# A first-chunk head for each pass, weights behind the input, head steps at slot ends, and one more product in 32 on GpSimd

## The chip, the cores and the metric

The kernel runs on one core of a Trainium2 chip. The core has TensorE (PE) for matmuls, VectorE (DVE), ScalarE (ACT) and GpSimd (POOL) for elementwise work, SyncE (SP) that here issues all DMAs, an on-chip memory of 128 partitions (SBUF), and eight PSUM banks into which TensorE writes. Each engine takes its own instructions in order. The metric is device time in microseconds, lower is better.

## The reference

Two layers on x of shape (1, 64, 256, 128) = (b, c, t, f). Layer 0 is a two-directional Mamba, first along t (each f is a sequence), then along f (each t is a sequence):

```python
def _mamba(u, p):
    x, z = split(u @ in_proj_w.T)                  # 128 channels each
    x = silu(causal_depthwise_conv4(x) + conv_b)
    dt, B, C = split(x @ x_proj_w.T, [4, 20])
    dt = softplus(dt @ dt_proj_w.T + dt_proj_b)
    A = -exp(A_log)                                # 128 channels x 16 states
    h[t] = exp(dt[t] * A) * h[t-1] + dt[t] * B[t] * x[t]
    y[t] = sum_s h[t] * C[t] + x[t] * Dp
    return (y * silu(z)) @ out_proj_w.T
def _block(u, p): return _mamba(rmsnorm(u, norm_w), p) + u
xt = xt + concat(block_fwd(xt), flip(block_bwd(flip(xt)))) @ tlin_w + tlin_b
xf = xf + concat(block_fwd(xf), flip(block_bwd(flip(xf)))) @ flin_w + flin_b
```

Layer 1 is a global layer norm and a two-directional convolutional LSTM over windows of 8 time steps, a transposed convolution, two PReLUs and a residual. Everything is float32.

## The kernel before

**Two passes and a third stage.** `Stage` runs twice (stage 0 along t, stage 1 along f); `ConvLstm` follows. Between them the whole tensor `X` (128 partitions x 128 x 128) stays in SBUF. A pass has 64 chunks of 512 tokens, each with two directions d. Of the 128 channels x 16 states, one 128x1024 tile holds an eighth (a "pair" of 128x512), so a chunk has 2 x 8 = 16 pairs. A pair is a **slot** S; there are 16 x 64 = 1024 slots in a pass and 2048 in all.

**What a slot does.** `inputs` (L445) spreads dt·x over states on TensorE into a PSUM tile `bx` (three buffers of two banks). `decays` (L462 to L468) computes exp(dt·A) into `dA` on ScalarE, from a tile `rep` to which a DMA of 512 KB (L420) has copied each channel's dt 16 times. `times_b` multiplies `bx` by B; `recur` is the scan on VectorE (L490); `outputs` multiplies by C on GpSimd (L503); `add_up` sums the states on TensorE into the bank `y` (L512). For most slots `times_b` is on VectorE (L480). For a slot in `SWAPPED` (modulo 32; there are seven) ScalarE first copies `bx` to the SBUF tile `dA` (L462), the decays go into the PSUM tile, and B is multiplied on GpSimd (L477). The edges of `dA` are set to zero by small ScalarE copies (L465) where a tile changes its role or its direction.

**The order.** `Stage.run` writes the order out by hand. In slot S it emits B for S+1, the scan of S, C for S-1, the spread for S+2, the decays for S+2 (at one slot S+2 and S+3), then the **head steps** listed for the slot in `HEAD`, then `add_up` of S-2 and, at slots 2 and 3 of a chunk, the closing products and `keep` of the chunk before.

**The head.** Everything that a chunk needs before its first scan is a list of steps with slots, relative to 16 slots before the chunk starts: load `u`, its squares, means and rms; `normalise` (GpSimd, L311), whose result four DMAs bring into the padded tile `unp` (L314); `project_x` and `project_z` for both directions; all silus together between two loads of ScalarE's function tables; `project_bc`, whose result goes out to DRAM (`away`) and comes back as B and C; softplus in three steps (`pv`, `e`, `w`, `lw`, summed by TensorE and copied to `dt`); `dt_away` and `spread_dt`, which bring it back as `rep`; `times_x`. All of the head's matmuls, the closing ones and `made` share one PSUM bank (`mm`, tag "mm"), which passes on when its reader is done. The first chunk of a pass takes the same steps with no slot beside them.

**The start.** `Mamba.__init__` (L160 to L229) loads all weights with 33 transfers and builds the matrices, `Gates.load` (L690 to L694) issues 9 more, and then the first chunk's `u` is loaded.

**`made`.** During chunks of the second pass, the response of the LSTM's input weights to the norm's gain and bias is computed: at slot 10, `fetch` loads 512 KB of weights, and at slot 6 of ten chunks `respond` (L707) multiplies them, 8 matmuls of 2 columns (16 instructions in the trace), and ScalarE copies the result (L710).

Of the kernel before, what the change touches and what calls it, by code (L numbers as in the profile page):

```python
# [37 lines left out]
C = 64  # L38
# [20 lines left out]
NREP = 7  # L59
NH = 5  # L60
LAG = 2
SWAPPED = (3, 5, 10, 14, 19, 26, 29)
# [7 lines left out]
    (-11, "load"),  # L70
    (-7, "squares"),
    (-5, "means"),
    (-5, "rms"),
    (-3, "normalise"),
    (0, "project_x", 0),
    (1, "project_z", 0),
    (4, "project_x", 1),
    (5, "project_z", 1),
    (5, "silus"),
    (6, "project_bc", 0),  # L80
    (8, "softplus_a", 0),
    (8, "softplus_b", 0),
    (10, "spread_bc", 0, 0),
    (10, "softplus_sum", 0),
    (12, "dt_away", 0),
    (12, "spread_bc", 0, 1),
    (12, "spread_dt", 0, 0),
    (12, "times_x", 0),
    (12, "spread_dt", 0, 1),
    (12, "project_bc", 1),  # L90
    (12, "spread_dt", 0, 2),
    (13, "softplus_a", 1),
    (13, "softplus_b", 1),
    (14, "spread_dt", 0, 3),
    (15, "spread_dt", 0, 4),
    (15, "softplus_sum", 1),
    (15, "spread_dt", 0, 5),
    (15, "spread_dt", 0, 6),
    (15, "spread_bc", 1, 1),
    (18, "dt_away", 1),  # L100
    (18, "spread_dt", 0, 7),
    (19, "spread_dt", 1, 0),
    (20, "spread_bc", 1, 0),
    (20, "spread_dt", 1, 1),
    (20, "times_x", 1),
    (22, "spread_dt", 1, 2),
    (22, "spread_dt", 1, 3),
    (23, "spread_dt", 1, 4),
    (26, "spread_dt", 1, 5),
    (27, "spread_dt", 1, 6),  # L110
    (27, "spread_dt", 1, 7),
# [3 lines left out]
class Mamba:  # L115


    def __init__(self, ctx, tc, d):
        nc = tc.nc
        self.nc, self.tc = nc, tc  # L120
        cp = ctx.enter_context(tc.tile_pool(name="m_const", bufs=1))

        self.ident = cp.tile([P, P], F32, name="ident")
        make_identity(nc, self.ident)

        mask = cp.tile([P, 2, NK, DL], F32, name="mask")
        flat = mask.rearrange("p r k d -> p (r k d)")
        nc.vector.tensor_add(flat, self.ident[:, 0:C], self.ident[:, C:P])  # L130
        self.sel = cp.tile([P, 2, NK, P], F32, name="sel")
        for r in range(2):
            for k in range(NK):
                nc.vector.tensor_copy(
                    self.sel[:, r, k].rearrange("p (s d) -> p s d", s=NS),
                    mask[:, r, k].unsqueeze(1).to_broadcast([P, NS, DL]),
                )
        self.fold = cp.tile([P, NK, 32], F32, name="fold")
        with tc.tile_pool(name="m_fold", bufs=1, space=PSUM) as ps:
            pf = ps.tile([P, NK, 32], F32, name="pf")  # L140
            for k in range(NK):
                nc.tensor.matmul(
                    pf[:, k], lhsT=self.sel[0:32, 0, k], rhs=self.ident[0:32, 0:32], start=True, stop=True
                )
            nc.vector.tensor_copy(self.fold, pf)


        self.ones = cp.tile([P, P], F32, name="ones")
        nc.vector.memset(self.ones, 0.0)
        for h in range(2):  # L150
            own = slice(h * C, (h + 1) * C)
            nc.vector.memset(self.ones[own, own], 1.0 / C)
        self.eps = cp.tile([P, 1], F32, name="eps")
        nc.vector.memset(self.eps, RMS_EPS)

        self.cb = cp.tile([P, 4], F32, name="cb")
        self.dtb = cp.tile([P, 4], F32, name="dtb")
        self.dp = cp.tile([P, 4], F32, name="dp")
        normw = cp.tile([C, 4], F32, name="normw")
        nc.sync.dma_start(out=self.cb, in_=d["conv_b"])  # L160
        nc.sync.dma_start(out=self.dtb, in_=d["dt_b"])
        nc.sync.dma_start(out=self.dp, in_=d["Dp"])
        nc.sync.dma_start(out=normw, in_=d["norm_w"])


        nc.scalar.preload_act_table_set(EXP_AND_LN)
        self.A = cp.tile([P, 4, NG], F32, name="A")
        nc.sync.dma_start(out=self.A, in_=d["A_log"])
        nc.scalar.activation(self.A, self.A, AF.Exp)
        nc.vector.tensor_scalar(self.A, self.A, -1.0, None, ALU.mult)  # L170

        self.G1, self.G2, self.Wz, self.Wdt, self.Wbc, self.W2 = ([] for _ in range(6))
        self.W3, self.lin_b = [], []
        with tc.tile_pool(name="m_prep", bufs=2) as pp, tc.tile_pool(
            name="m_prep_ps", bufs=2, space=PSUM
        ) as ps:
            lins = []
            for i, n in enumerate(("tlin", "flin")):
                lin = pp.tile([C, 2, C], F32, name=n, tag=n, bufs=1)
                nc.sync.dma_start(out=lin, in_=d[n + "_w"].rearrange("(h i) o -> i h o", h=2))  # L180
                lins.append(lin)
                b = cp.tile([C, 1], F32, name=n + "b", tag=n + "b")
                nc.sync.dma_start(out=b, in_=d[n + "_b"].rearrange("(c o) -> c o", o=1))
                self.lin_b.append(b)

                w3 = cp.tile([P, 2, C], F32, name=f"w3{i}", tag=f"w3{i}")
                nc.vector.memset(w3, 0.0)
                nc.vector.tensor_add(w3[0:C, 0], lin[:, 0], lin[:, 1])
                nc.vector.tensor_add(w3[0:C, 0], w3[0:C, 0], self.ident[0:C, 0:C])
                nc.vector.tensor_copy(w3[C:P, 1], w3[0:C, 0])  # L190
                self.W3.append(w3)

            for i in range(4):
                win = pp.tile([C, 2 * P], F32, name="win", tag="win")
                nc.sync.dma_start(out=win, in_=d["in_proj"][i])
                cw = pp.tile([C, 4, P], F32, name="cw", tag="cw")
                nc.sync.dma_start(out=cw, in_=d["conv_w"][i].partition_broadcast(C))
                xpd = pp.tile([RANK, P], F32, name="xpd", tag="xpd")
                nc.sync.dma_start(out=xpd, in_=d["x_proj_dt"][i])
                dtw = pp.tile([RANK, P], F32, name="dtw", tag="dtw")  # L200
                nc.sync.dma_start(out=dtw, in_=d["dt_proj"][i])
                xbc = cp.tile([P, NBC], F32, name=f"xbc{i}", tag=f"xbc{i}")
                nc.sync.dma_start(out=xbc, in_=d["x_proj_bc"][i])
                self.Wbc.append(xbc)
                ow = pp.tile([C, P], F32, name="ow", tag="ow")
                nc.sync.dma_start(out=ow, in_=d["out_proj"][i])

                nc.vector.tensor_scalar(win, win, normw[:, i : i + 1], None, ALU.mult)
                wz = cp.tile([C, P], F32, name=f"wz{i}", tag=f"wz{i}")
                nc.vector.tensor_copy(wz, win[:, P : 2 * P])  # L210
                self.Wz.append(wz)

                taps = ((3, 2), (1, 0)) if i % 2 == 0 else ((2, 3), (0, 1))
                for j, keep in enumerate((self.G1, self.G2)):
                    g = cp.tile([P, P], F32, name=f"g{j}{i}", tag=f"g{j}{i}")
                    nc.vector.tensor_mul(g[0:C], win[:, 0:P], cw[:, taps[j][0]])
                    nc.vector.tensor_mul(g[C:P], win[:, 0:P], cw[:, taps[j][1]])
                    keep.append(g)

                pw = ps.tile([P, P], F32, name="pw", tag="pw")  # L220
                nc.tensor.matmul(pw, lhsT=xpd, rhs=dtw, start=True, stop=True)
                wdt = cp.tile([P, P], F32, name=f"wdt{i}", tag=f"wdt{i}")
                nc.vector.tensor_copy(wdt, pw)
                self.Wdt.append(wdt)

                po = ps.tile([P, C], F32, name="po", tag="po")
                nc.tensor.matmul(po, lhsT=ow, rhs=lins[i // 2][:, i % 2], start=True, stop=True)
                w2 = cp.tile([P, C], F32, name=f"w2{i}", tag=f"w2{i}")
                nc.vector.tensor_copy(w2, po)  # L229
                self.W2.append(w2)  # L230


class Stage:
# [8 lines left out]
    def __init__(self, ctx, m, stage, L, X, src, moments, gates):  # L242
# [24 lines left out]
        self.at = {}  # L267
# [8 lines left out]
    def mm(self, name):  # L276
        return self.ps_mm.tile([P, NTOK], F32, name=name, tag="mm")
# [40 lines left out]

    def project_x(self, ch, d):
        nc, m, L = self.nc, self.m, self.L  # L320
        i = 2 * self.stage + d
        first, second = (3, 1) if d == 0 else (4, 6)
        px = self.mm("px")
        xs = self.wk.tile([P, NTOK], F32, name="xs", tag="xs", bufs=3)
        nc.tensor.matmul(self.seqs(px), lhsT=m.G1[i], rhs=self.unp[:, :, first : first + L], start=True, stop=False)  # L325
# [99 lines left out]
    def head(self, ch):  # L425
        todo = {}
        for slot, name, *args in HEAD:
            todo.setdefault(slot, []).append((getattr(self, name), (ch, *args)))
# [736 lines left out]
```

## Time and profile before

| | |
|---|---|
| median of three runs | 7435.62 us (7434.42 to 7440.39) |
| the profiled execution | 7439.22 us, span 7437.4 us |
| busy: PE, DVE, ACT, POOL | 6526, 6987, 6000, 6559 us |
| first scan of the first pass | 72.0 us after the start |
| last scan of the first pass, first of the second | 3338.2 (two in a row, 4.45 us), 3395.3 us |
| last scans of the second pass | 6739.9 us (two in a row, 4.45 us) |
| end | 7437.4 us |

A line of a group gives line, engine, operation, tiles and shapes, the count, then the busy time in us and the mean in ns, then the engine's idle time just before and who ended it. A line of a table of stretches gives from, to and length in us, the busy time of each engine with its instructions, the TensorE clock that was granted (1.00 is full speed), the DMA engines' busy share, and GB/s. A line of waits gives who waited for whom, us in total, times, and the longest. A line of the timeline gives start and duration in us, engine, line, operation, and in brackets the idle time before it and who ended it.

An engine's instructions overlap a little at their ends, so that the distance between two starts is somewhat less than the mean duration: a scan with B behind it starts 2.20 us before that B (2000 to 2110 us), though its row says 2.27.

### The profile page before, as it was taken

To read this page: it belongs to the slowest core of one execution; us is meant where nothing else is said; L and a number is where in the kernel's file an instruction comes from. 1 tells how busy PE (TensorE), PEld (TensorE's weight loads), DVE (VectorE), ACT (ScalarE), POOL (GpSimd) and SP (SyncE) were. 2 spreads that over 40 slices of the span, in tenths; PEclk is the share of its full clock that TensorE was granted. 3 is DMA by queue.
4 is the path that set the end of the run, shared out by engine and by line. 5 is a ranking of instruction groups with operands and counts; after the bars stand their busy time and mean duration, and the time that the engine had idled before them with its cause. 6 is when DMAs were issued, how large, how long until landed. Compare 5 with 4: busy or idle time off the path is not lost. (4 is left out here: it accounts for less than half of the span.)

```text
span 7437.4 us, 86153 instructions
## 1 busy us (share of the span) xinstructions
PE 6526.3 (88%) x25104; PEld 2203.8 (30%) x25104; DVE 6987.4 (94%) x4740; ACT 5999.8 (81%) x10892; POOL 6558.7 (88%) x3348
## 2 busy tenths in 40 slices
PE   7888888888888888887888888888888888888999
PEld 2222222222222222222222222222222222225887
DVE  6999999999999999996888999999999999996887
ACT  6888888888888888877777889888888888884333
POOL 5999999999999999996888999999999999995554
PEclk9999999999999999998999999999999999999999
DMA  5887888887888888876777877777777878782000
GB/s 148 207 208 205 205 210 204 207 207 202 206 207 204 206 205 205 206 185 163 190 184 186 204 201 202 203 208 201 201 204 202 208 197 205 205 203 72 15 15 16
DMA packets 509540, 1359.97 MB, mean 183 GB/s; under 512 B 75376, under 2 KB 133392, under 8 KB 509072
## 3 DMA queue, kind: packets, MB, share of 16 engines
q1 hardware_dynamic: 509072, 1354.46, 71.4%
q8 instruction: 205, 3.36, 0.2%
q14 instruction: 263, 2.15, 0.1%
HBM read 1228.34 MB, written 92.27 MB: 178 GB/s over the span
## 5 line engine op out<-in xcount | busy, mean ns | idle before, releaser
L503 POOL TENSOR_TENSOR h<-h,C 128x1024 f32<-128x1024 f32 x2048 | 4795.1, 2367 | 137.7 <-DVE h L490 120.1
L490 DVE TENSOR_TENSOR_SCAN h<-dA,bx 128x1024 f32<-128x1024 f32 x1600 | 3602.3, 2271 | 7.7 <-ACT dA L468 7.7
L445 PE MATMUL bx<-dtx,sel 64*128 64x512 f32 x8192 | 2368.3, 654 | 205.9 <-DVE h L490 205.7
L480 DVE TENSOR_TENSOR bx<-bx,B 128x1024 f32<-128x1024 f32 x1600 | 1940.8, 1213 | 251.0 <-PE bx L445 250.7
L468 ACT ACTIVATE dA<-rep,A 128x510 f32<-128x510 f32 (+1 forms) x3200 | 2117.0, 710 | 9.2 <-DMA rep<-there 6.0
L477 POOL TENSOR_TENSOR dA<-dA,B 128x1024 f32<-128x1024 f32 x448 | 1057.0, 2359 | 294.1 <-ACT dA L462 284.5
L445 PEld LDWEIGHTS bx<-dtx,sel 64*128 64x128 f32 x8192 | 640.4, 188 | 1857.4 <-issue 1045.8
L512 PE MATMUL y<-h,fold 128*32 128x512 f32 x8192 | 1119.0, 614 | 14.3 <-POOL h L503 7.6
L490 DVE TENSOR_TENSOR_SCAN h<-bx,dA 128x1024 f32<-128x1024 f32 x448 | 1021.0, 2279 | 2.5 <-POOL dA L477 1.3
L462 ACT COPY dA<-bx 128x1024 f32<-128x1024 f32 x448 | 450.7, 1006 | 251.3 <-PE bx L445 251.3
L468 ACT ACTIVATE bx<-rep,A 128x510 f32<-128x510 f32 (+1 forms) x896 | 617.4, 689 | 29.4 <-ACT bx L465 0.2
L401 PE MATMUL pb<-xs,xbc 128*32 128x512 f32 x512 | 291.4, 654 | 287.8 <-ACT xs L349 239.5
L327 ACT ACTIVATE xs<-px,cb 128x512 f32<-128x512 f32 x256 | 175.9, 687 | 372.9 <-PE px L326 372.9
L512 PEld LDWEIGHTS y<-h,fold 128*32 128x32 f32 x8192 | 167.3, 109 | 788.3 <-issue 432.0
L395 POOL TENSOR_TENSOR dtx<-dt,xs 128x512 f32<-128x512 f32 x256 | 326.8, 1276 | 62.2 <-ACT dt L383 62.2
L325 PE MATMUL px<-unp,g 128*128 128x512 f32 x512 | 292.7, 653 | 78.2 <-ACT X L561 35.8
L379 PE MATMUL pv<-w,ident 128*128 128x512 f32 x512 | 276.9, 623 | 91.1 <-ACT w L371 91.1
L358 PE MATMUL pv<-xs,wdt 128*128 128x512 f32 x512 | 290.0, 648 | 67.1 <-ACT bc L403 59.4
L379 PE MATMUL pv<-e,ident 128*128 128x512 f32 x512 | 290.0, 648 | 11.1 <-ACT e L362 7.8
L332 PE MATMUL pz<-unp,wz 64*128 64x512 f32 x512 | 268.2, 603 | 3.2 <-ACT xs L327 3.1
L326 PE MATMUL px<-unp,g 128*128 128x512 f32 x512 | 266.2, 601 | 0.0
L379 PE MATMUL pv<-lw,ident 128*128 128x512 f32 x512 | 262.7, 595 | 0.0
(190 smaller groups left out, 6887.6 us busy)
## 6 DMA issues: line engine op xcount, KB each, us to landing
rep<-there SPq DMA_DIRECT2D x2048, 512.0 KB
B<-away SPq DMA_DIRECT2D x256, 256.0 KB
there<-dt SPq DMA_DIRECT2D x1024, 64.0 KB
C<-away SPq DMA_DIRECT2D x256, 256.0 KB
unp<-xn SPq DMA_DIRECT2D x512, 64.0 KB
away<-bc SPq DMA_DIRECT2D x256, 64.0 KB
u<-in_x SPq DMA_DIRECT2D x128, 64.0 KB
out<-y SPq DMA_DIRECT2D x32, 256.0 KB
```

What stands on the lines that cost most here:

```text
L325: nc.tensor.matmul(self.seqs(px), lhsT=m.G1[i], rhs=self.unp[:, :, first : first + L], start=True, stop=False)
L379: nc.tensor.matmul(pv, lhsT=self.m.ident, rhs=t, start=False, stop=n == len(parts) - 1, skip_group_check=True)
L395: self.nc.gpsimd.tensor_mul(dtx, self.at["dt", d], self.at["xs", ch, d])
L401: self.nc.tensor.matmul(pb, lhsT=self.m.Wbc[2 * self.stage + d], rhs=self.at["xs", ch, d], start=True, stop=True)
L445: self.nc.tensor.matmul(bx[:, j], lhsT=self.m.sel[rows, r, k], rhs=dtx[rows], start=True, stop=True)
L462: nc.scalar.copy(dA.rearrange("p j n l -> p j (n l)"), bx)
L468: nc.scalar.activation(dA[:, j, :, live], self.seqs(rep[:, j])[:, :, live], AF.Exp, scale=m.A[:, i, g : g + 1])
L477: self.nc.gpsimd.tensor_mul(bx, bx, b)
L480: self.nc.vector.tensor_mul(bx, bx, b)
L490: self.nc.vector.tensor_tensor_scan(h.rearrange("p j n -> p (j n)")[:, step], dA[:, step], bx[:, step], 0.0, ALU.mult, ALU.add,)
L503: self.nc.gpsimd.tensor_mul(h, h, self.at["C", ch, d].unsqueeze(1).to_broadcast([P, 2, NTOK]))
L512: nc.tensor.matmul(y[32 * r : 32 * r + 32], lhsT=m.fold[:, k], rhs=hs[r % 2][:, r // 2], start=False, stop=k == NK - 1, skip_group_check=True,
```

## The change

- **Slots that give B to GpSimd:** eight of 32 instead of seven, now the same in every chunk (2, 5, 9, 14).
- **The head's slots** are listed anew, and a step may stand at a half slot: it is then emitted at the end of the slot, behind `add_up` and the closing products.
- **The first chunk of each pass** has its own head, `first`. It uses six PSUM banks (the three `bx` tiles) beside the shared one; `normalise_here` writes `unp` straight from VectorE with no DMA; silu is applied from PSUM as the first direction's x appears; direction 0's x, dt, B and C are made first, then direction 1's x and both z. The rest of direction 1 is in `SECOND`, whose slots run from 14 of the head to 17.
- **Weights** come in ten transfers, five behind the first `u`, five after the normalisation's instructions. They lie in `X` until the first chunk's result is stored there. The matrices are built in pieces between the head's steps. Small columns are one tensor, `cols`.
- **`made`:** each of the ten sets is split into two, four matmuls each, at slot 6 of twenty chunks; its fetch moves to slot 6.

```diff
-SWAPPED = (3, 5, 10, 14, 19, 26, 29)
+SWAPPED = (2, 5, 9, 14, 18, 21, 25, 30)
 HEAD = (
-    (-11, "load"),
-    (-7, "squares"),
-    (-5, "means"),
-    (-5, "rms"),
+    (-13, "load"),
+    (-8.5, "squares"),
+    (-4.5, "means"),
+    (-4.5, "rms"),
     (-3, "normalise"),
     (0, "project_x", 0),
-    (1, "project_z", 0),
-    (4, "project_x", 1),
-    (5, "project_z", 1),
+    (1.5, "project_z", 0),
+    (4, "project_z", 1),
+    (5, "project_x", 1),
     (5, "silus"),
-    (6, "project_bc", 0),
+    (7.5, "project_bc", 0),
     (8, "softplus_a", 0),
-    (8, "softplus_b", 0),
-    (10, "spread_bc", 0, 0),
-    (10, "softplus_sum", 0),
-    (12, "dt_away", 0),
+    (8.5, "softplus_b", 0),
+    (8.5, "spread_bc", 0, 0),
+    (10.5, "softplus_sum", 0),
+    (10.5, "dt_away", 0),
+    (11.5, "times_x", 0),
 ...
+    def load(self, first):
+        dma, d = self.nc.sync.dma_start, self.d
+        if first:
+            dma(out=self.win[:, 0], in_=d["in_proj"][:, 0])
+            dma(out=self.cw[:, 0], in_=d["conv_w"][0].partition_broadcast(C))
+            dma(out=self.cols, in_=d["cols"])
+            dma(out=self.xdt, in_=d["dt_proj"])
+            dma(out=self.Wbc, in_=d["x_proj_bc"])
+        else:
+            dma(out=self.win[:, 1:4], in_=d["in_proj"][:, 1:4])
+            dma(out=self.cw[:, 1:4], in_=d["conv_w"][1:4].partition_broadcast(C))
+            dma(out=self.lin, in_=d["lin_w"])
+            dma(out=self.b, in_=d["lin_b"])
+            dma(out=self.ow, in_=d["out_proj"])
 ...
     def mm(self, name):
+        if self.spare:
+            return self.spare.pop(0)
         return self.ps_mm.tile([P, NTOK], F32, name=name, tag="mm")
 ...
+    def normalise_here(self):
+        nc, n, L = self.nc, self.nseq // 2, self.L
+        for h in range(2):
+            own = slice(h * C, (h + 1) * C)
+            for to in range(2):
+                nc.vector.tensor_mul(
+                    self.unp[to * C : (to + 1) * C, h * n : (h + 1) * n, 3 + to : 3 + to + L],
+                    self.at["u", 0][own],
+                    self.rs[own],
+                )
 ...
+    def first(self):
+        nc, m = self.nc, self.m
+        s, time = 2 * self.stage, self.time
+        banks = [self.ps_bx.tile([P, 2, NTOK], F32, name="bx", tag="bx") for _ in range(3)]
+        self.load(0)
+        if time:
+            m.load(True)
+        self.squares(0)
+        if time:
+            m.shifts(0)
+        self.means(0)
+        self.rms(0)
+        nc.scalar.preload_act_table_set(SILU)
+        self.normalise_here()
+        if time:
+            m.dt(0, self.mm("pw"))
+            m.load(False)
 ...
+        self.shifted(banks[0][:, 0], s)
+        nc.scalar.activation(x[0], banks[0][:, 0], AF.Silu, bias=m.cb[:, s : s + 1])
+        nc.scalar.preload_act_table_set(EXP_AND_LN)
+        self.softplus_a(0, 0)
+        if time:
+            m.decay()
+            m.spreads()
+            m.gates(0)
+            m.shifts(1)
+            m.gates(1)
+        self.softplus_b(0, 0)
+        self.spare = [banks[0][:, 1]]
+        self.project_bc(0, 0)
+        self.spread_bc(0, 0, 0)
+        self.softplus_sum(0, 0)
+        self.dt_away(0, 0)
+        self.times_x(0, 0)
+        for n in range(4):
+            self.spread_dt(0, 0, n)
+            if n == 0:
+                self.spread_bc(0, 0, 1)
+        if time:
+            m.dt(1, self.mm("pw"))
+        self.shifted(banks[1][:, 0], s + 1)
+        for d in range(2):
+            self.gated(banks[1 + d][:, 1], s + d)
+        nc.scalar.preload_act_table_set(SILU)
+        nc.scalar.activation(x[1], banks[1][:, 0], AF.Silu, bias=m.cb[:, s + 1 : s + 2])
+        for d in range(2):
+            nc.scalar.activation(z[d], banks[1 + d][:, 1], AF.Silu)
+        nc.scalar.preload_act_table_set(EXP_AND_LN)
+        self.spare = [banks[2][:, 0]]
+        self.project_bc(0, 1)
+        if time:
+            m.folds(self.mm("pf"))
+            for i in (2, 3):
+                m.shifts(i)
+                m.gates(i)
+                m.dt(i, self.mm("pw"))
+            for n in range(2):
+                m.residual(n)
+            for i in range(4):
+                m.closing(i, self.mm("pc"))
 ...
-        for S in range(min(steps), last + LAG + 4):
+        self.first()
+        for S in range(int(min(steps)), last + LAG + 4):
 ...
+            for f, args in steps.get(S + 0.5, []):
+                f(*args)
 ...
-                if n < 10 and S % 16 == 10:
-                    self.gates.fetch(n, self.io)
-                if 0 < n < 11 and S % 16 == 6:
-                    self.gates.respond(n - 1, self.mm("made"))
+                if S % 16 == RESPOND:
+                    if 0 < n < 21:
+                        self.gates.respond(*divmod(n - 1, 2), self.mm("made"))
+                    if n < 20 and n % 2 == 0:
+                        self.gates.fetch(n // 2, self.io)
```

In `Mamba`, `shifts(i)` is five VectorE operations of up to 64x256, `gates(i)` one copy, `dt(i)` a matmul and a copy, `spreads` nine operations, `folds` four matmuls and a copy, `residual(n)` three operations of 64x64, `closing(i)` a matmul and a copy; they are the operations of L130 to L229 of before.

## The prediction

> **What bounds the kernel now.** I read the table of stretches first. In the first and the second pass alike:
>
> ```profile
> core 0: us, PE busy (x) PEld busy (x) DVE busy (x) ACT busy (x) POOL busy (x), PEclk, DMA share, GB/s
> 2000.00:3000.00 1000.00, 884.32 (x3330) 241.69 (x3332) 984.38 (x597) 870.68 (x1553) 949.83 (x442) 0.99 0.82 206
> ...
> 5000.00:6000.00 1000.00, 880.43 (x3326) 241.53 (x3324) 982.73 (x596) 882.51 (x1628) 949.67 (x441) 0.99 0.80 203
> ```
>
> VectorE is busy for 98% of both, GpSimd for 95%, TensorE and ScalarE for 88%: VectorE sets the pace, and GpSimd stands close behind. The groups of instructions give their work:
>
> ```profile
> L503 POOL TENSOR_TENSOR h<-h,C 128x1024 f32<-128x1024 f32 x2048 | 4795.1, 2367 | 137.7 <-DVE h L490 120.1
> L490 DVE TENSOR_TENSOR_SCAN h<-dA,bx 128x1024 f32<-128x1024 f32 x1600 | 3602.3, 2271 | 7.7 <-ACT dA L468 7.7
> ...
> L480 DVE TENSOR_TENSOR bx<-bx,B 128x1024 f32<-128x1024 f32 x1600 | 1940.8, 1213 | 251.0 <-PE bx L445 250.7
> ...
> L477 POOL TENSOR_TENSOR dA<-dA,B 128x1024 f32<-128x1024 f32 x448 | 1057.0, 2359 | 294.1 <-ACT dA L462 284.5
> ```
>
> Every pair (slot) has one scan on VectorE and one product with C on GpSimd; the product with B is VectorE's in 25 of 32 slots and GpSimd's in 7. From 130 to 3300 us there are 994 slots, 3.19 us each, or 102.05 us for 32 (102.4 in the second pass). What VectorE still waits for, from 130 to 3300 us, from 3500 to 4100 and from 4100 to 6700:
>
> ```profile
> DVE bx L480 <- PE bx L445: 43.1, 109, 1.8
> ...
> DVE bx L480 <- PE bx L445: 70.5, 33, 7.1
> ...
> DVE bx L480 <- PE bx L445: 41.7, 85, 1.8
> ```
>
> That is 1.36% and 1.6% of the outer stretches, but 12% of the middle one, whose longest wait is 7.1 us. The timeline shows one such wait:
>
> ```profile
> 3528.59 0.57 ACT L403 COPY bc<-pb 32x512 f32<-32x512 f32 x1
> ...
> 3529.22 3.57 PE L707 MATMUL made<-gb,w 128*128 128x2 f32 x16 [2.40 <-ACT bc L403]
> ...
> 3532.72 2.08 PE L445 MATMUL bx<-dtx,sel 64*128 64x512 f32 x4
> ...
> 3534.84 1.23 DVE L480 TENSOR_TENSOR bx<-bx,B 128x1024 f32<-128x1024 f32 x1 [7.11 <-PE bx L445]
> ```
>
> `made` needs the one spare bank that `pb` holds until ScalarE, behind two table loads and four silus, has copied `bc`. TensorE takes its queue in order, so `bx` stands behind that wait and behind 3.57 us of `made`. Last, where VectorE has nothing to do:
>
> ```profile
> 24.58 1.11 SPq L288 DMA_DIRECT2D u<-in_x  x2
> ...
> 60.68 0.58 ACT L383 COPY dt<-pv 128x512 f32<-128x512 f32 x1 [3.02 <-PE pv L379]
> ...
> 72.02 2.29 DVE L490 TENSOR_TENSOR_SCAN h<-dA,bx 128x1024 f32<-128x1024 f32 x1 [3.08 <-ACT dA L468]
> ...
> 3350.24 0.42 ACT L295 ACTIVATE sq<-X 128x256 f32<-128x256 f32 x1
> ...
> 3395.33 2.29 DVE L490 TENSOR_TENSOR_SCAN h<-dA,bx 128x1024 f32<-128x1024 f32 x1 [2.42 <-ACT dA L468]
> ```
>
> The first scan comes at 72.0 us, and in the second pass 45.1 us after the squares. The LSTM layer behind the passes (about 690 us, bound by TensorE) isn't touched.
>
> **Start of the first pass.** Before `u`, SyncE issues 42 small loads, until 24.5 us. Now `u` goes first and ten loads follow. A `u` takes 3.1 us from issue (24.58) to squares (27.71), so it is there at 3.9. From there I add durations of the old head's rows. Table load 1.28 and squares 0.42: 5.6. Means 1.25, first `rs` 0.5: 7.4. The opening load of the Exp/Ln table is gone, so the order of ScalarE has loads before Square, Ln and Exp; Ln's lies beside the means, Exp's 1.28 with its 0.42 is on the path: 9.1. Four VectorE products of 64x256 replace the GpSimd product, four DMAs and their landing (30.44 to 35.16, 4.7 us); no row has this shape, 64x128 takes 0.28 and 128x512 0.67, so some 0.4 each: 10.6. Two shifted products at the slow clock of 35.19 to 38.98, 3.8: 14.4. Silu 0.7, `pv` 2.07 (the table load lies beside it), three activations 2.0, `decay` 0.26 and the next three 1.9: 21.3. From the last of those to `dt` the old head takes 3.9: 25.2, against 61.3.
>
> The old scan came 10.8 us after `dt`; here ScalarE and TensorE are late instead. Behind `dt` stand the second direction's products (3.8 slow, then 2.2 for z): 31.3. Then `pb` and folds, 2: 33.3. The fold, two Wdt and four W2 products share one bank, each with about 0.7 of matmul, 0.3 of copy and the hand-over; VectorE's shifts for weights 2 and 3 (1.75 each) and the residual (six, 1.2) stand between them: some 10, 43.3. Only then come chunk 1's means and rs (2.2), which stand ahead of the first decays (1.5) on ScalarE: about 47. Best is 36, where the `rep` transfer alone decides (25.2 + 10.8); worst I put at 57, with that tail doubled. **-25 us** (-36 to -15). The ten loads lie beside the head; if one were late it would hold `shifts`, which is inside this range.
>
> **Start of the second pass.** The same path without loads and weights, from the squares: 0.45, means and rs 1.7, products 1.5, shifted 3.8, silu 0.7, `pv` 2.1, activations 3.9, to `dt` 3.9: 18.1 (34.4 before). Then z and its silus, two table loads, `bc`, chunk 1's rs and the decays, about 12: 30 against 45.1. **-15 us** (-20 to -8).
>
> **`made`.** Before: ten times 16 matrix instructions at slot 6, behind `pb`. Now `pb` is at 7.5, the bank's last user at slot 6 is `px`, and each of 20 chunks has 8 of the 16. At the second pass's usual 1.6%, 600 us would have 9.7 us of waits instead of 70.5: 61 us to win. Eight instructions take half of 3.57, 1.8 us; VectorE needs a `bx` one scan and one B (3.3) after its buffer came free, and 1.13 of matmul with some 0.5 of hand-over lies in that: 1.6 us of slack, so I charge 1 us of stall, 20 in all (nothing to 2.3 us each, the latter as dear per matmul as now). The 512 KB fetches move from slot 10 to slot 6 on SyncE, in front of later `rep` issues; there are still ten. **-40 us** (-15 to -60).
>
> **One more B in 32 on GpSimd.** Consecutive starts in the timeline give what an operation costs its engine: B 1.115 us on VectorE (2003.36 to 2004.47), 2.31 on GpSimd. Per 32 slots:
> - VectorE: 98.44% of 102.05 = 100.5 busy, less 1.12: 99.3.
> - GpSimd: 94.98% = 96.9, plus 2.31: 99.2.
> - ScalarE: one copy (1.006) and two zero copies (0.19) more, 88.9 to 90.2.
>
> VectorE stays just ahead. If its idle time stays at 1.6, 32 slots take 100.9, in which GpSimd has 1.7 us to spare instead of 5.1. 64 groups by 1.12: **-71 us**.
>
> [...] GpSimd's row is 2359 ns beside 1213 ns. [...] Taken for the sum of engine time, 64 times (2.31 - 1.12) would be 76 us lost. The stretches show the engines side by side and GpSimd idle for 5.1 us in 32 slots, so I take the row. [...]
>
> **Head steps at slot ends.** A half slot puts a step behind the slot's `y` and closing products on TensorE; on SyncE the transfers of `dt`, `rep`, B and C move by up to three slots with their steps, and wait there in the new order. Instructions and bytes are the same, so only VectorE's 1.4 us per 32 can shrink or grow. In the old slots they fall on B of slots 6, 7 and 9, behind swapped 3 and 5; the new pattern repeats 2, 5, 9, 14 in each chunk. I can't work out a sign: 0, with -0.7 to +0.7 per group, -45 to +45.
>
> **Sum.** -25 - 15 - 40 - 71 = -151 on the span of 7437.4: 7286. The profiled execution as a whole was 7439.2, the median of the three runs 7435.6, so 3.6 less than profiled: with 1.8 around the span, 7284.6 to the median **7281 us**.
>
> **Rivals.**
> 1. *GpSimd becomes half a bound.* From 130 to 3300 us it waits so:
>
> ```profile
> POOL dA L477 <- ACT dA L462: 102.9, 153, 2.0
> POOL h L503 <- DVE h L490: 40.3, 57, 1.2
> ```
>
> For: 99.2 and 99.3 are equal, and any wait left on GpSimd is then paid by VectorE. Against: those waits fall where GpSimd runs early; one that lags absorbs them. If half the gain of the steady slots goes, with a little stall on TensorE too, -20 instead of -71: 7332.
> 2. *The other sign: GpSimd keeps its waits.* 102.9 us in 217 swapped slots is 0.47 each, 3.8 for 8, and 1.3 for h: 99.2 + 3.8 + 1.3 = 104.3 per 32 slots, 2.3 more than now, +145; less the 80 of heads and `made`: about 7500. It decides from 3.9 us of idle left on GpSimd (80/64 = 1.25 on top of 102.05). Against: the ScalarE copy follows a scan by about 3 us, and a lagging GpSimd comes later.
> 3. *The waits on TensorE go too.* Steps behind the slot's other products leave `bx` early, and `made` is hidden: another 45 + 15: 7221.
> 4. *The head changes nothing*, as the weights are still awaited: 40 us less gain, 7321; the ten loads behind the input speak against it.
>
> **How the numbers follow.** Forecast 0.58, rival 1 0.18, rival 2 0.05, rival 3 0.14, rival 4 0.05. Without rival 2 the parts' bounds and rivals 1 and 3 reach from about 7205 to 7355, which holds 8 in 10. A measurement of this kernel tells 0.2% (15 us) from no change: faster 0.93, same 0.02, slower 0.05.
>
> **What would show it.** First scan near 47 us; about 30 us from the second pass's squares to its scan; L707 in 20 blocks of 1.8 us and no VectorE wait over 3 us from 3400 to 4600; 1536 B on VectorE and 512 on GpSimd; 32 slots in about 101 us, with VectorE and GpSimd both above 97% busy. I am wrong if VectorE's scans wait for `dA` of GpSimd (L477's successor) by more than 1 us in 32 slots, or if its waits for `bx` grow beyond 2 us.

## The result, and the profile after

The changed kernel takes **7324.3 us** (median of four runs, 7317.7 to 7326.2) against 7435.0 before (four runs, 7433.3 to 7440.4): a ratio of 0.985, 95% interval 0.983 to 0.987. The forecast was 7281, so it is 111 us instead of 154. The span went from 7437.4 to 7324.0. Cut at the first and last scans of both passes, the 113.4 us lie here:

| part | before | after | gain | forecast |
|---|---|---|---|---|
| to the first scan | 72.0 | 48.7 | 23.3 | 25 |
| first pass, first to last scan | 3270.7 | 3272.8 | **-2.1** | some 36 (half of 71) |
| last scan to first scan of the second pass | 52.6 | 35.2 | 17.4 | 15 |
| second pass | 3349.0 | 3275.2 | 73.8 | 40 + some 36 |
| behind the passes | 693.1 | 692.1 | 1.0 | 0 |

Both starts came near their forecasts. In the first pass, which has no `made`, the product that was moved to GpSimd brought nothing. That the second pass's 73.8 us lie so near the 76 of the forecast is luck: some 69 of them are `made`'s, for which 40 had been forecast, and only some 5 are left for the product.

The names in what follows: `px`, `pz` and `pb` are the TensorE products of `project_x`, `project_z` and `project_bc`, `bc` is the copy of `pb` on ScalarE, `pv` is the product of `softplus_a`, and `yz` is y times silu(z), one for each direction of a chunk. In the changed kernel's code B on VectorE is L588, B on GpSimd L585, the scan L598, `bx` L553, `pv` L398, the copy of `bc` L443 and `yz` L636. The groups show that the product was moved:

```profile
L611 POOL TENSOR_TENSOR h<-h,C 128x1024 f32<-128x1024 f32 x2048 | 4797.5, 2366 | 32.4 <-DVE h L598 22.0
L598 DVE TENSOR_TENSOR_SCAN h<-dA,bx 128x1024 f32<-128x1024 f32 x1536 | 3443.8, 2269 | 0.0
...
L588 DVE TENSOR_TENSOR bx<-bx,B 128x1024 f32<-128x1024 f32 x1536 | 1863.7, 1213 | 178.8 <-PE bx L553 178.2
...
L585 POOL TENSOR_TENSOR dA<-dA,B 128x1024 f32<-128x1024 f32 x512 | 1205.9, 2355 | 161.9 <-ACT dA L570 155.8
```

The table of stretches, in the middle of the first pass and of the second:

```profile
2000.00:3000.00 1000.00, 885.80 (x3336) 253.84 (x3334) 977.21 (x589) 894.02 (x1589) 973.52 (x452) 0.98 0.84 206
5000.00:6000.00 1000.00, 884.12 (x3314) 250.59 (x3306) 972.85 (x585) 902.72 (x1658) 970.14 (x450) 0.97 0.82 203
```

GpSimd rose from 95 to 97%, but VectorE *fell* from 98.4 to 97.7%: it does less and waits more. Its waits from 130 to 3300 us are all for one thing, and none is for GpSimd:

```profile
DVE bx L588 <- PE bx L553: 73.5, 103, 1.6
```

It was 43.1 us there before. What makes `bx` late is seen in one chunk's timeline, TensorE first, then VectorE:

```profile
2022.65 1.13 PE L553 MATMUL bx<-dtx,sel 64*128 64x512 f32 x4 [0.34 <-DVE h L598]
2025.62 1.90 PE L398 MATMUL pv<-xs,wdt 128*128 128x512 f32 x2 [1.84 <-ACT bc L443]
2027.45 2.00 PE L553 MATMUL bx<-dtx,sel 64*128 64x512 f32 x4
```
```profile
2025.87 2.29 DVE L598 TENSOR_TENSOR_SCAN h<-bx,dA 128x1024 f32<-128x1024 f32 x1
2029.50 1.23 DVE L588 TENSOR_TENSOR bx<-bx,B 128x1024 f32<-128x1024 f32 x1 [1.34 <-PE bx L553]
```

`pv` waits 1.84 us for the shared bank, until ScalarE has copied `bc`. Then `pv` takes 1.90 us and the next `bx` 2.00. In another chunk of the same pass, with the same wait, they take 1.12 and 1.13, and VectorE's B follows its scan at once:

```profile
3250.59 1.12 PE L398 MATMUL pv<-xs,wdt 128*128 128x512 f32 x2 [1.83 <-ACT bc L443]
3251.64 1.13 PE L553 MATMUL bx<-dtx,sel 64*128 64x512 f32 x4
```
```profile
3250.84 2.29 DVE L598 TENSOR_TENSOR_SCAN h<-bx,dA 128x1024 f32<-128x1024 f32 x1
3253.05 1.21 DVE L588 TENSOR_TENSOR bx<-bx,B 128x1024 f32<-128x1024 f32 x1
```

The difference is the granted clock (the third number from the end) in short stretches of the first of them:

```profile
2024.00:2026.00 2.00, 0.38 (x1) 0.33 (x2) 2.00 (x3) 1.97 (x6) 2.00 (x2) 0.96 0.00 0
2026.00:2028.00 2.00, 2.00 (x4) 0.51 (x4) 2.00 (x1) 1.64 (x3) 2.00 (x1) 0.50 0.45 129
2028.00:2030.00 2.00, 2.00 (x12) 0.16 (x8) 0.66 (x2) 1.97 (x4) 2.00 (x2) 0.69 1.01 248
```

Half clock for about 3.4 us (0.16 + 2 + 1.24, from 0.96, 0.50 and 0.69). To count this I take a chunk as the time from one `yz` to the second next, with its mean clock. The chunks of the first pass:

| | at full clock | at a lower clock (0.93 to 0.97) | mean of all |
|---|---|---|---|
| before | 38 of 50.68 us | 22 of 51.81 us | 51.09 |
| after | 19 of 50.18 us | 41 of 51.55 us | 51.11 |

At full clock a chunk did get 0.50 us shorter, near the 0.56 that half of 1.12 makes. But twice as many chunks lose the clock.

### The profile page after: what moved, and what is told of

The parts are those of the page before. It is cut to its first block, busy times and chain, and to the rows that moved or that the text cites. A ratio compares the mean times of both kernels' runs of the same rounds, so it can differ in the third digit from the quotient of the medians.

```text
span 7324.0 us, 86482 instructions
## 1 busy us (share of the span) xinstructions
PE 6510.4 (89%) x25104; PEld 2254.8 (31%) x25104; DVE 6924.8 (95%) x4684; ACT 6119.2 (84%) x11092; POOL 6703.3 (92%) x3410
## 5 line engine op out<-in xcount | busy, mean ns | idle before, releaser
L598 DVE TENSOR_TENSOR_SCAN h<-dA,bx 128x1024 f32<-128x1024 f32 x1536 | 3443.8, 2269 | 0.0
L553 PE MATMUL bx<-dtx,sel 64*128 64x512 f32 x8192 | 2578.7, 653 | 364.8 <-DVE h L598 362.5
L588 DVE TENSOR_TENSOR bx<-bx,B 128x1024 f32<-128x1024 f32 x1536 | 1863.7, 1213 | 178.8 <-PE bx L553 178.2
L576 ACT ACTIVATE dA<-rep,cols 128x510 f32<-128x510 f32 (+1 forms) x3072 | 2021.7, 710 | 11.3 <-DMA rep<-there 11.3
L585 POOL TENSOR_TENSOR dA<-dA,B 128x1024 f32<-128x1024 f32 x512 | 1205.9, 2355 | 161.9 <-ACT dA L570 155.8
L553 PEld LDWEIGHTS bx<-dtx,sel 64*128 64x128 f32 x8192 | 733.3, 190 | 1888.1 <-issue 1070.5
L620 PE MATMUL y<-h,fold 128*32 128x512 f32 x8192 | 1239.5, 618 | 12.6 <-POOL h L611 10.9
L598 DVE TENSOR_TENSOR_SCAN h<-bx,dA 128x1024 f32<-128x1024 f32 x512 | 1167.9, 2281 | 15.4 <-POOL dA L585 15.4
L576 ACT ACTIVATE bx<-rep,cols 128x510 f32<-128x510 f32 (+1 forms) x1024 | 705.5, 689 | 33.7 <-ACT bx L573 0.4
L398 PE MATMUL pv<-xs,wdt 128*128 128x512 f32 x512 | 341.2, 753 | 261.5 <-ACT bc L443 167.5
L441 PE MATMUL pb<-xs,wbc 128*32 128x512 f32 x504 | 260.9, 599 | 15.6 <-ACT made L809 15.6
```

Source lines behind the costliest of these rows:

```text
L398: nc.tensor.matmul(pv, lhsT=m.Wdt[i], rhs=self.at["xs", ch, d], start=True, stop=True)
L553: self.nc.tensor.matmul(bx[:, j], lhsT=self.m.sel[rows, r, k], rhs=dtx[rows], start=True, stop=True)
L576: nc.scalar.activation(dA[:, j, :, live], self.seqs(rep[:, j])[:, :, live], AF.Exp, scale=m.A[:, i, g : g + 1])
L585: self.nc.gpsimd.tensor_mul(bx, bx, b)
L588: self.nc.vector.tensor_mul(bx, bx, b)
L598: self.nc.vector.tensor_tensor_scan(h.rearrange("p j n -> p (j n)")[:, step], dA[:, step], bx[:, step], 0.0, ALU.mult, ALU.add,)
```

## The experiments

Medians of four runs each; a ratio is to the kernel before, which took 7435 to 7437 us beside them. None of them changes what is computed.

| run | us | ratio, 95% interval | first-pass chunk, mean us |
|---|---|---|---|
| changed kernel | 7324.3 | 0.983 to 0.987 | 51.11 |
| `pv9` | 7235.2 | 0.972 to 0.974 | 50.21 |
| `warm` | 7313.7 | 0.982 to 0.985 | 50.79 |
| `warm2` | 7249.0 | 0.973 to 0.976 | 50.22 |
| `seven` | 7302.7 | 0.980 to 0.984 | 50.98 |
| `seven_pv9` | 7395.3 | 0.993 to 0.996 | 51.52 |
| `b8` | 7580.8 | 1.018 to 1.021 | 52.26 |
| `b8_pb7` | 7600.8 | 1.021 to 1.024 | 52.52 |
| `old_early` | 7574.4 | 1.017 to 1.020 | 52.26 |
| `old_late` | 7350.3 | 0.987 to 0.991 | 51.13 |
| `xz_old` | 7401.4 | 0.994 to 0.997 | 51.53 |
| `made_whole` | 7336.5 | 0.985 to 0.989 | 51.05 |
| `sum11` | 7326.4 | 0.983 to 0.986 | 50.85 |

**Is it pv's wait, and is it the clock?** First `pv` out of the way of `bx`:

```diff
-    (8, "softplus_a", 0),
-    (8.5, "softplus_b", 0),
+    (9, "softplus_a", 0),
+    (9, "softplus_b", 0),
```

> The changed kernel with softplus_a and softplus_b of direction 0 at slot 9 instead of 8 and 8.5, so that pv stands in TensorE's queue behind the bx of slot 11 and no bx waits with it for ScalarE's copy of bc. Theory 1 (the wait of pv and the clock drop that follows it): the 66 slow chunks of some 1.35 us each get rarer, 40 to 80 us faster than the changed kernel, about 7265; granted clock above 0.985. Theory 2 (GpSimd is the bound): within 15 us of 7324. Theory 3 (the gap on TensorE stays, because bx of slot 11 has to wait for a buffer too): the clock stays at 0.97 and at most 20 us are won.

It is 89 us faster than the changed kernel. No chunk of the first pass is below full clock; 57 of 62 take 50.15 to 50.18 us. VectorE is at 99.5%, and GpSimd, which one expectation took for the bound, at 98.9%:

```profile
2000.00:3000.00 1000.00, 900.00 (x3395) 254.16 (x3394) 994.84 (x598) 904.31 (x1615) 989.41 (x459) 1.00 0.85 210
```

This moves the order and the clock together. So next the order stays and TensorE gets *more* to do, ahead of `pv`: products with zeros as weights, added into `y`, three of them in `warm` and two in `warm2`, which is shown:

```diff
         i = 2 * self.stage + d
+        if d == 0 and ch > 0:
+            for _ in range(2):
+                nc.tensor.matmul(
+                    self.y[0:32], lhsT=m.ones[0:C, C : C + 32], rhs=self.at["dtx", ch - 1, 1][0:C],
+                    start=False, stop=False, skip_group_check=True,
+                )
         pv = self.mm("pv")
```

> The changed kernel with three more matrix products of 64x512 per chunk ahead of pv of direction 0, with a block of zeros as weights, added into y: 1.7 us of work more for TensorE in the gap of 1.84 us in which it waits for bc; the output doesn't change. Theory 1 (the gap lowers the clock, the low clock makes bx late): although TensorE has 124 x 1.7 = 210 us more to do, the time falls by 40 to 80 us, to about 7265, and the granted clock rises from 0.975 to over 0.985. Theory 2 (GpSimd is the bound): within 15 us of 7324. Theory 3 (it is the order of the queue alone, and not the clock): no gain, or up to 60 us slower.

> The changed kernel with two instead of three products of zeros ahead of pv per chunk: four matrix instructions that took 0.46 us each with three, so 1.84 us, just the length of the wait for bc; with three they took 2.76 us, and VectorE then waited 0.49 us for bx in each chunk. Theory 1 (the gap costs time through the clock alone; the order of pv and bx costs nothing while the clock is full): the chunks become the good ones, 50.2 and 50.5 us, and the time comes close to 7240. Theory 2 (the order costs, whatever the clock): no better than with three, 7313 within 15 us, chunks of 50.7 us.

With three products (six instructions in the trace) the clock was full in every chunk of the first pass (mean of the whole run 0.994), yet only 11 us were won: the six instructions took 2.76 us where the wait was 1.84, and VectorE now waited 0.49 us for `bx` in each chunk. My expectation had put them at 1.7 us. With two, which fit the wait, the timeline of TensorE is this:

```profile
2037.03 1.13 PE L559 MATMUL bx<-dtx,sel 64*128 64x512 f32 x4 [0.34 <-DVE h L604]
2038.09 1.90 PE L399 MATMUL y<-dtx,ones 64*32 64x512 f32 x4
2039.98 1.12 PE L404 MATMUL pv<-xs,wdt 128*128 128x512 f32 x2
2041.03 1.13 PE L559 MATMUL bx<-dtx,sel 64*128 64x512 f32 x4
```

`pv` and `bx` stand at the same distance from the `bx` before as they did (2.95 and 4.00 us here, 2.96 and 4.01 at full clock in the changed kernel), but always at full clock. TensorE has 118 us more to do in the first pass alone, and the kernel is **75 us faster**. So this wait in the queue cost nothing by itself; what it cost was the clock.

**What is the eighth B worth?** The old seven slots in the changed kernel (`seven`, shown), the new eight in the kernel before (`b8`), and the seven with `pv` at 9 (`seven_pv9`):

```diff
-SWAPPED = (2, 5, 9, 14, 18, 21, 25, 30)
+SWAPPED = (3, 5, 10, 14, 19, 26, 29)
```

> The changed kernel with the seven swapped slots of before (3, 5, 10, 14, 19, 26, 29); all else stays. Theory 1 (the eighth B pays its 1.12 us in every 32 slots, and the head steps at slot ends give about as much back, as TensorE stands idle ahead of pv and its granted clock falls to 0.5): without the eighth B the time rises by 64 x 1.12 = 71 us, to about 7395, and the good chunks of 50.2 us become 50.7. Theory 2 (GpSimd is the bound of the changed kernel): its busy share falls from 97 to 95% and the time stays within 20 us of 7324, or falls.

> The kernel before with the eight swapped slots of the change (2, 5, 9, 14, 18, 21, 25, 30) alone; heads, weights and made as before. Theory 1 (the eighth B is worth its VectorE time, what was lost comes from the order of the head steps): 71 us faster than before, about 7364, and nearer 50.2 than 50.7 us for a good chunk. Theory 2 (GpSimd is the bound as soon as it has eight): no gain, 7435 within 20 us, as in the first pass of the changed kernel.

> The changed kernel with pv at slot 9 and the seven swapped slots of before. Theory 1 (with the wait of pv gone the eighth B is worth its VectorE time, as forecast): 64 x 1.12 = 71 us slower than with eight, about 7306, chunks of 50.7 us. Theory 2 (GpSimd, busy for 98.9% with eight, is the bound there): at most 25 us slower than with eight, about 7255.

All three missed. In the changed kernel the eight made it 22 us *slower*: with seven, a chunk at full clock takes 50.61 us instead of 50.18, but 40 of 61 chunks have full clock, not 19 of 60. In the kernel before, the eight cost 145 us. With `pv` at 9 they are worth 160 us, not 71. So the new list of slots has no value of its own: it is worth -145, -22 or +160 us, as the head's steps stand. (The list changes the places of the old seven along with their number, 3 to 2 or 10 to 9; no run parts the two. And the 160 include clock: with seven, a third of the chunks lost it again.) In `b8` the clock is not the main reason: a chunk at full clock takes 52.0 to 52.2 us there too, against 50.68 in the kernel before. VectorE waits for GpSimd and GpSimd for ScalarE's copy of `bx`, from 130 to 3200 us:

```profile
DVE bx L480 <- PE bx L445: 76.1, 158, 1.6
DVE h L490 <- POOL dA L477: 45.9, 46, 1.3
...
POOL dA L477 <- ACT dA L462: 109.3, 86, 2.3
```

Why `seven_pv9` is slower than `seven` was not settled; some 20 of its 61 chunks are below full clock, and those at full clock take 51.26 us.

**Which head steps let GpSimd take eight?** I took `pb` for the cause, which in the old order waits 1.76 us for a silu with `bx` behind it.

```diff
-    (6, "project_bc", 0),
-    (8, "softplus_a", 0),
-    (8, "softplus_b", 0),
-    (10, "softplus_sum", 0),
+    (7, "project_bc", 0),
+    (9, "softplus_a", 0),
+    (9, "softplus_b", 0),
+    (11, "softplus_sum", 0),
```

> The kernel before with the eight swapped slots, and in its old head pb at slot 7 (from 6), softplus at 9 (from 8) and its sum at 11 (from 10), whole slots all. Theory 1 (the eight cost 145 us there because bx stands on TensorE behind pb, which waits 1.76 us for a silu, and GpSimd's B then starts late): chunks fall from 52.3 to below 51 us; with made now ahead of pb, the time falls from 7581 to about 7380. Theory 2 (GpSimd's own waits for ScalarE's copies cost it, whatever stands on TensorE): only made's part comes, some 50 us, and chunks stay above 52 us: about 7530.

With `pb`, softplus and its sum each one slot later, it is 20 us slower than `b8`: the place of `pb` alone is not it. So I split the head of the changed kernel: in `old_early` the steps up to `softplus_sum` of direction 0 stand in the slots of before, in `old_late` those from `dt_away` on.

> The changed kernel (eight swapped slots) with the head steps up to softplus_sum of direction 0 in the slots of before (squares -7, means -5, pz at 1 and 5, px at 4, pb at 6, softplus at 8, its sum at 10), the later steps as changed. Theory 1 (in the old head the eight B's suffer from the early steps on TensorE: px, pz, pb and pv stand ahead of bx with waits for ScalarE): the first pass's chunks stay near the 52.3 us of the eight in the old head, and the time near 7330 + 124 x 0.9, about 7440 (a little more where made stands behind pb again). Theory 2 (it is the later steps, which put dt, dtx and the reps away): chunks at 50.2 to 51.6 us as in the changed kernel, about 7324 to 7370.

> The reverse: the changed kernel with the steps from dt_away of direction 0 on in the slots of before (dt_away and times_x at 12, pb of direction 1 at 12, dt_away 18, times_x 20, the reps between), the early ones as changed. Theory 1 (early steps): chunks of 50.2 to 51.6 us as in the changed kernel, about 7324 within 30 us. Theory 2 (later steps): chunks near 52.3 us, about 7440.

The early steps carry it wholly: `old_early` has the very chunk of `b8`, 52.26 us, `old_late` that of the changed kernel. My estimate of 7440 for `old_early` was too low: beside 1.15 us a chunk it gets back the wait of `made` behind `pb` (chunks of 56.9 us in that stretch). Then `pv9` with `squares`, `means`, `rms`, `px` and `pz` in the slots and order of before:

```diff
-    (-8.5, "squares"),
-    (-4.5, "means"),
-    (-4.5, "rms"),
+    (-7, "squares"),
+    (-5, "means"),
+    (-5, "rms"),
...
-    (1.5, "project_z", 0),
-    (4, "project_z", 1),
-    (5, "project_x", 1),
+    (1, "project_z", 0),
+    (4, "project_x", 1),
+    (5, "project_z", 1),
```

> The changed kernel with pv at slot 9, and with squares, means, pz and px in the slots and order of before (squares -7, means and rms -5, pz of direction 0 at 1, px at 4, pz at 5); pb stays at 7.5 and the sum at 10.5. It splits the early steps in two. Theory 1 (with eight on GpSimd it is the early pb that costs, which waits 1.76 us for a silu ahead of bx): chunks stay near 50.2 us and the time within 25 us of 7235. Theory 2 (it is px, pz and the means): chunks of 52 us or more, about 7480.

Between both: chunks of 51.5 us, at full clock or not. These steps are worth 1.3 of the 2.05 us between 50.21 and 52.26; by subtraction, the rest goes with the other early ones (`pb`, softplus, its sum), which were not parted. VectorE now waits for GpSimd, and GpSimd for ScalarE's copy of `bx` (25.9 us with the new slots), from 130 to 3200 us:

```profile
DVE h L598 <- POOL dA L585: 52.3, 60, 0.9
...
POOL dA L585 <- ACT dA L570: 97.9, 137, 1.3
```

**`made`, place or split?** Ten chunks with all 16 instructions at slot 6 (`respond` again makes both halves; that part of the edit is left out here):

```diff
-                    if 0 < n < 21:
-                        self.gates.respond(*divmod(n - 1, 2), self.mm("made"))
+                    if 0 < n < 21 and n % 2:
+                        self.gates.respond(n // 2, self.mm("made"))
 ...
```

> The changed kernel with the sets of made not split: ten chunks with 16 matrix instructions and one copy at slot 6, instead of twenty with 8. Theory 1 (what was won is the place ahead of pb, where nothing holds the bank): within 20 us of 7324. Theory 2 (what was won is the split): some 3 us of wait in each of ten chunks comes back, and the ten chunks that now have none of it fall to the slow clock more often; 30 to 45 us slower, about 7360.

12 us more, with intervals of the ratio that overlap: the split is worth 12 us at most, and the rest of what `made` gave goes with its place. Being ahead of `pb` is not enough, though. In `b8_pb7` `made` is ahead of it as well, waits for nothing and takes 1.95 us, and yet its ten chunks take 57.1 us each against 52.8 of the others: `pb` one slot later then waits up to 1.9 us for ScalarE's copy of `made`, which stands behind the silus. There the fetch was also still at slot 10; no run moves it alone.

**How full is GpSimd?** In `pv9`, the sum of softplus and `dt_away` go to slot 11 instead of 10.5, to take a wait from TensorE:

> The changed kernel with pv at slot 9, and its softplus_sum and dt_away at 11 instead of 10.5, so that TensorE no longer waits for w there (49.7 us in the first pass with pv at 9). Theory 1 (VectorE waits for next to nothing any more, 16 us in the first pass, and GpSimd is busy for 98.9%): within 12 us of 7235. Theory 2 (bx still suffers from that wait): 15 to 30 us faster, about 7212.

Both theories missed: it is 91 us slower than `pv9`. The copy `dt` comes later now, and GpSimd, which has `dtx` to make from it, waits some 1.1 us in every chunk (from 130 to 3200 us):

```profile
POOL dtx L435 <- ACT dt L423: 66.5, 61, 1.1
```

With `pv9` GpSimd idles for 1.1% of a chunk, 0.5 us. The chunk became 0.64 us longer, about what the wait takes beyond that slack.

## Why the prediction was right and wrong, by its steps

- **Start of the first pass: right, as two errors nearly cancel.** First scan at 48.7 us (47 forecast). The last W2 copy ended at 39.8, 3.5 earlier than the 43.3 of the forecast, and the ten loads did lie beside the head. From there to the scan it took 8.9 us, not 3.7. A transfer that the sum left out came last: chunk 1's `u`, issued at 31.9 behind the `rep` fetches on SyncE, so that its squares, which stand ahead of the first decays, began at 40.80; that is about 1 us. The sum also had nothing for the first two `bx` with a `pv` between them (42.42 to 47.43, of which 42 to 46.3 at a granted clock of 0.52) and the B of the first slot (1.2).
- **Start of the second pass: right.** 27.4 us from squares (3329.33) to scan (3356.72), 30 forecast.
- **`made`: mechanism right, size off.** Its ten chunks took 580.8 us, 69 more than ten plain ones of that pass (51.17), where the sum began with 61. After, the twenty take no more than others. "I charge 1 us of stall" was the term: eight instructions took 1.05 us, not 1.8, which is within the slack of 1.6. They were priced from the row of 3.57 us, which ran at half clock: from 3529 to 3533 us the granted clock was 0.50. At full clock the same 16 take 1.95 us (`made_whole`).
- **One more B in 32, -71, with head steps at slot ends, 0: here the forecast failed.** The sum took VectorE's waits as a constant 1.6 us in 32 slots, and said of the half slots that they could move it by 0.7 at most. The waits for `bx` rose from 41.6 to 73.2 us in 130 to 3200, which is 1.05 us in 32 slots, nearly the whole of the 1.12 to be won. With 2.4 us in 32 slots they passed the 2 us that were named as a sign of being wrong. The step that failed is that "0": the new slots put a wait of 1.84 us on TensorE into every chunk, and the sum has no term for what a wait on TensorE does to its clock. `pv9` and `warm2` show this: 89 and 75 us come back, with chunks of 50.2 us where the forecast's 100.9 for two make 50.45. The profile before had it, too: a clock of 0.99 in its stretches, which I took for full, was 38 chunks of 1.00 and 22 of 0.97 that each took 1.13 us more.
- **Adding the two was wrong as well.** I took the head's new slots as worth nothing to GpSimd. With the old head the eight cost 145 us (`b8`), and the changed kernel with the old early steps is 250 us slower (`old_early`, in part by `made`'s wait). The last line of the sum has a slip besides: 151 off the median of 7435.6 makes 7284.6, and 7281 takes the 3.6 us between the profiled execution and the median off twice.
- **Rivals.** Two have nearly the measured time, 7324, by another cause. The first is GpSimd as half a bound (7332): in the first pass VectorE waits for GpSimd nowhere, and `pv9` wins 89 us though GpSimd has as much to do. The fourth is a head that changes nothing (7321): the two starts gave 23.3 and 17.4 us. The second's sum, 104.3 us for 32 slots, is what `b8` measured (2 x 52.26 = 104.5): it was right for the old head, and wrong for the changed one. The third (waits on TensorE go too, 7221) is close to what `pv9` makes of the change, 7235.
- **Room on GpSimd.** A second such move was not tried; but with one, at 98.9% (`pv9`), a wait of 1.1 us in each chunk already lengthens the chunk by 0.64 us (`sum11`).

## What to carry to other kernels

Price a wait on a nearly full TensorE twice: by what stands behind it, and by the clock that it may lose (here half of it for 3.4 us or more, behind 41 of 60 such waits); read the granted clock chunk by chunk, since a mean of 0.99 hid a third of the chunks at 0.97. Where a clock drop is suspected, give TensorE idle work that fits into the wait and see that nothing else moves: if the kernel gets faster with more work, it was the clock (`warm2`: 118 us more work in the first pass, 75 us faster). Work that was longer than the wait gave most of it back (`warm`: 2.76 us in a wait of 1.84, 11 us won instead of 75). And a move of work to a second engine that is then 99% full has no price apart from the order of everything that this engine waits for: try it with each order, since here the same list of slots was worth -145 and +160 us.

## What the runs showed of the hardware

In the first pass of the changed kernel a wait of 1.84 us on TensorE, with 0.34 us of idle time shortly before, was followed by half clock in 41 of 60 chunks, for 3.4 us or, eight times, for 6.8; in the others the same wait was not. In `pv9`, where 2056 to 2058 us has 1.20 us of idle time, and in `warm2`, with products in the wait, every chunk of the first pass had a clock of 1.00.

The trace of the changed kernel shows what parts the two kinds of chunk. From 130 to 3260 us each of its 42 stretches of half clock is 3.413 us long or twice that, and all changes of the clock in the run lie whole multiples of 3.413 us apart (within 0.02 us). Here are two steps of this length around the slow chunk above, and three around a wait of the same length in a chunk at full clock; the first number behind the length is TensorE's busy time:

```profile
2022.41:2025.83 3.41, 1.34 (x5) 0.52 (x6) 3.41 (x3) 3.32 (x7) 3.33 (x3) 1.00 0.01 1
2025.83:2029.24 3.41, 3.41 (x6) 0.62 (x5) 2.33 (x2) 3.05 (x7) 3.41 (x3) 0.50 0.65 169
...
2787.00:2790.41 3.41, 2.21 (x13) 0.47 (x12) 3.41 (x2) 3.31 (x5) 3.33 (x2) 1.00 0.93 218
2790.41:2793.83 3.41, 2.44 (x7) 0.73 (x8) 3.41 (x3) 3.41 (x8) 3.41 (x2) 1.00 0.31 98
2793.83:2797.24 3.41, 3.41 (x15) 1.12 (x14) 3.41 (x4) 3.32 (x8) 3.41 (x3) 1.00 1.05 236
```

In the slow chunk one step holds 2.07 us of idle time, and the next step has half clock. In the other the wait (2789.6 to 2791.4) lies in two steps, which have 1.20 and 0.97 us, and the next has a clock of 1.00. From 130 to 3260 us TensorE was idle for more than 1.76 us in 43 steps at full clock, and 41 of them were followed by half clock; of the 819 with less than 1.72 us none was. (The chunk at 3250 us is one of the two exceptions, with 1.83 us.) So in this trace it was the place of the wait in these steps that parted the two kinds of chunk, not its length. The trace of before shows them less cleanly parted: from 130 to 3300 us 30 steps at full clock have 1.86 us of idle time each, and 22 of them were followed by half clock, the other eight not. What else parts those was not shown.
